# A window attention and Fourier layer over 32 images: image entry, data layout and instruction order redone

## The chip, the cores and the metric

The kernel runs on one core of one Trainium2 chip. The metric is the device time in microseconds (us) of one execution; a lower time is better. TensorE's granted clock is given as a mean over the run, 1.0 being full speed.

## The reference, cut to what matters

```python
# x: (32, 56, 56, 128) fp32, 32 images of 56 x 56 pixels, 128 channels
x = x + attention(group_norm(x), rpb_table, w_qkv, w_proj, b_proj)
x = x + fourier(group_norm(x), w0, w1, W1, b1, W2, b2)

def attention(x):            # Swin, shifted by 3
    xs  = roll(x, (-3, -3))  # windows of 7 x 7, so 8 rows of 8 windows in an image
    q, k, v = windows(xs) @ w_qkv.T           # 4 heads of 32
    a   = softmax(q @ k.T * scale + bias + mask)
    return roll(a @ v @ w_proj.T + b_proj, (3, 3))

def fourier(x):
    xy = idct(mix(dct(x, along width)[:32],  w0))   # 32 modes, a 128x128 matrix for each
    xx = idct(mix(dct(x, along height)[:32], w1))
    return relu((xx + xy) @ W1 + b1) @ W2 + b2       # hidden size 512
```

The attention of an image has to end before its second group norm, and so before its Fourier layer. What can run beside each other is the Fourier layer of one image and the attention of the next. Everything is fp32, and the biases are zeros in the inputs.

## The kernel before

Image entry: transpose 28 pieces, take statistics, then let GpSimd write normalised windows in 27 pieces (cut).

```python
def image_in(b):
    ...                                    # 28 TensorE transposes, ScalarE copies to xT
    rstd, nb = group_stats(st, 0)
    xw = big.tile([P, NWR, NWR, WS, WS], F32, tag="xw", name="xw")
    for i in range(NWR):
        for r0, r1, y0 in rolled(i):
            for j0, j1, s0, s1, x0 in (...):          # the roll cuts the windows
                nc.gpsimd.tensor_scalar(xw[:, i, j0:j1, r0:r1, s0:s1], xT[...], rstd, nb,
                                        ALU.mult, ALU.add)
```

One row of eight windows: K is written into a block-diagonal tile by four copies, each of one head (32 partitions), alternating between ScalarE and VectorE. The score matmul takes all 128 partitions.

```python
    for h in range(NH):
        hs = slice(h * HD, (h + 1) * HD)
        if h % 2:
            nc.vector.tensor_copy(k_bd[hs, :, h], pk3[hs])
        else:
            nc.scalar.copy(k_bd[hs, :, h], pk3[hs])
    ...
    nc.tensor.matmul(ps[half * JP : ..., ...], lhsT=q[:, w * WT : w * WT + JP],
                     rhs=k_bd[:, w].rearrange("c h j -> c (h j)"), ...)   # 196 columns
```

The Fourier layer is a generator whose steps are put between the parts of attention. Columns are made by a GpSimd copy and TensorE transposes (cut):

```python
    for q in range(4):
        nc.gpsimd.tensor_copy(xh[:, ws], xT[:, :, ws].rearrange("p h w -> p w h"))
    for width in (False, True):
        ...                                   # per group: 4 transposes, ScalarE copy, 8 dct matmuls
        nc.vector.tensor_scalar(y[:, 0], y[:, 0], shift, None, ALU.add)
        if width:
            nc.gpsimd.tensor_tensor(xtok, xtok, b2sb..., ALU.add)     # 112 x 3584 at once
        ...                                   # mixing, transposes of z, inverse into xf
    for g in range(NG):                       # feed-forward, 7 groups
        ...

    for b in range(NB):
        attn_scores(xw, 0)
        for i in range(NWR):
            conv = advance(conv, 4)           # 4 steps of the last image's Fourier layer
            if i + 1 < NWR:
                attn_scores(xw, i + 1)
            conv = advance(conv, 4)
            attn_out(xT, i)
        conv = advance(conv, 1000)
        conv = conv_layer(b, xT)
        if b + 1 < NB:
            xT, xw = image_in(b + 1)
```

Of the kernel before, what the change touches and what calls it, by code (L numbers as in the profile page):

```python
# [15 lines left out]
P = 128  # L16
S = 56
C = 128
WS = 7
SS = 3  # L20
NH = 4
# [13 lines left out]
JP = 64  # L35

HALVES = (slice(0, P // 2), slice(P // 2, P))
SQRT_S = float(np.sqrt(float(S)))


@with_exitstack
def swin_fourier_kernel(
# [27 lines left out]
    psum = ctx.enter_context(tc.tile_pool(name="psum", bufs=2, space=bass.MemoryType.PSUM))  # L70

    def bank(tag, bufs):
        return psum.tile([P, 512], F32, tag=tag, name=tag, bufs=bufs)
# [7 lines left out]
    x_tok_src = x.rearrange("b h w c -> b (h w) c").rearrange("b (n p) c -> b p n c", p=TC)  # L81
    out_tok_dst = out.rearrange("b h w c -> b (h w) c").rearrange("b (n p) c -> b p n c", p=TC)


    def load_image(b):
        t = big.tile([TC, NCH, C], F32, tag="xload", name="xload")
        h = NCH // 2
        nc.sync.dma_start(t[:, :h], x_tok_src[b, :, :h])
        nc.sync.dma_start(t[:, h:], x_tok_src[b, :, h:])
        return t  # L90

    loaded = {0: load_image(0)}
# [7 lines left out]
    make_identity(nc, ident)  # L100
    gavg = const_load([P, P], group_avg, "gavg")
    wqkv = const_load([P, 3 * C], w_qkv_t, "wqkv")
    wproj = const_load([P, C], w_proj_t, "wproj")
    bproj = const_load([P, 1], b_proj.rearrange("(c u) -> c u", u=1), "bproj")
# [19 lines left out]
    bm = const.tile([P, 2, 3, NH, WT], F32, tag="bm", name="bm")  # L124
    rpb_f = rpb.rearrange("p h y x -> p h (y x)")
    for r in range(2):
        for s in range(3):
            nc.vector.tensor_tensor(
                bm[:, r, s],
                rpb_f,  # L130
                mask_sb[:, r, s].unsqueeze(1).to_broadcast([P, NH, WT]),
                ALU.add,
            )

    dct_sb = const_load([TC, 2 * NM], dct, "dct")
    w0sb = const_load([P, NM, C], w0, "w0sb")
    w1sb = const_load([P, NM, C], w1, "w1sb")

# [3 lines left out]
    with nc.allow_non_contiguous_dma(reason="constant, once"):  # L142
        for li, ls in enumerate(HALVES):
            nc.scalar.dma_start(idctw[ls], idct_w[ls, li * 2 * S : (li + 1) * 2 * S])
            nc.scalar.dma_start(
                idcth[ls],
                idct_h.rearrange("p (h r) -> p h r", r=4)[ls, :, 2 * li : 2 * li + 2],
            )
    idcth = idcth.rearrange("p h r -> p (h r)")
    wff1 = const_load([P, FF], W1, "wff1")  # L150
# [5 lines left out]


    k_bd = big.tile([P, NWR, NH, WT], F32, tag="k_bd", name="k_bd")
    nc.gpsimd.memset(k_bd, 0.0)
    q_sb, v_bd, a_sb = [], [], []  # L160
    for i in range(2):
        q_sb.append(big.tile([P, RT + JP - WT], F32, tag=f"q{i}", name=f"q{i}"))
        v_bd.append(big.tile([P, NWR, 2, 2, HD], F32, tag=f"v{i}", name=f"v{i}"))
        a_sb.append(big.tile([P, NWR // 2, NH, JP], F32, tag=f"a{i}", name=f"a{i}"))
        nc.gpsimd.memset(q_sb[i], 0.0)
        nc.gpsimd.memset(v_bd[i], 0.0)
        nc.gpsimd.memset(a_sb[i], 0.0)

    def group_stats(st, n):

        mv = small.tile([P, 2], F32, tag="mv", name="mv")
        nc.vector.bn_aggr(mv, st)
        pg = attn_bank() if n == 0 else conv_bank()
# [9 lines left out]
        pv = attn_bank() if n == 0 else conv_bank()  # L183
# [3 lines left out]
        rstd = small.tile([P, 1], F32, tag=f"rstd{n}", name=f"rstd{n}")  # L187
        nc.gpsimd.tensor_tensor(rstd, ve, mhalf, ALU.pow)
        nb = small.tile([P, 1], F32, tag=f"nb{n}", name=f"nb{n}")
# [3 lines left out]
        return rstd, nb  # L193

    def rolled(i):

        y = WS * i + SS
        if i < NWR - 1:
            return ((0, WS, y),)
        return ((0, WS - SS, y), (WS - SS, WS, 0))  # L200


    def image_in(b):

        xl = loaded.pop(b)
        xT = big.tile([P, S, S], F32, tag="xT", name="xT", bufs=2)
        st = small.tile([P, NG, 6], F32, tag="st0", name="st0", bufs=2)
        for g in range(NG):
            pt = attn_bank()
            for i in range(4):  # L210
                nc.tensor.transpose(
                    pt[:, i * TC : (i + 1) * TC], xl[:, 4 * g + i], ident[:TC, :TC]
                )
            nc.vector.bn_stats(st[:, g], pt[:, :GT])
            nc.scalar.copy(
                xT[:, 8 * g : 8 * g + 8].rearrange("p r w -> p (r w)"), pt[:, :GT]
            )
        if b + 1 < NB:
            loaded[b + 1] = load_image(b + 1)
        rstd, nb = group_stats(st, 0)  # L220
        xw = big.tile([P, NWR, NWR, WS, WS], F32, tag="xw", name="xw")
        for i in range(NWR):
            for r0, r1, y0 in rolled(i):
                for j0, j1, s0, s1, x0 in (
                    (0, NWR - 1, 0, WS, SS),
                    (NWR - 1, NWR, 0, WS - SS, S - WS + SS),
                    (NWR - 1, NWR, WS - SS, WS, 0),
                ):
                    cols = (j1 - j0) * (s1 - s0)
                    nc.gpsimd.tensor_scalar(  # L230
                        xw[:, i, j0:j1, r0:r1, s0:s1],
                        xT[:, y0 : y0 + r1 - r0, x0 : x0 + cols].rearrange(
                            "p r (j s) -> p j r s", s=s1 - s0
                        ),
                        rstd,
                        nb,
                        ALU.mult,
                        ALU.add,
                    )
        return xT, xw  # L240


    def attn_scores(xw, i):

        q, v, a = q_sb[i % 2], v_bd[i % 2], a_sb[i % 2]
        src = xw[:, i].rearrange("p j r s -> p (j r s)")
        pq = attn_bank()
        nc.tensor.matmul(pq[:, :RT], lhsT=wqkv[:, 0:C], rhs=src, start=True, stop=True)  # L248
        nc.scalar.mul(q[:, :RT], pq[:, :RT], HD ** (-0.5))
        pk = attn_bank()  # L250
        nc.tensor.matmul(pk[:, :RT], lhsT=wqkv[:, C : 2 * C], rhs=src, start=True, stop=True)
        pk3 = pk[:, :RT].rearrange("p (w j) -> p w j", j=WT)
        for h in range(NH):
            hs = slice(h * HD, (h + 1) * HD)
            if h % 2:
                nc.vector.tensor_copy(k_bd[hs, :, h], pk3[hs])  # L256
            else:
                nc.scalar.copy(k_bd[hs, :, h], pk3[hs])  # L258
        pv = attn_bank()
        wv = wqkv[:, 2 * C : 3 * C].rearrange("c (p h d) -> c h p d", h=2, d=HD)  # L260
# [15 lines left out]
        t = work.tile([P, 2, 2, NH * WT], F32, tag="t", name="t")  # L276
        for hf in range(2):
            ps = attn_bank()
            for w4 in range(4):
                w = 4 * hf + w4  # L280
                half = w % 2
                nc.tensor.matmul(  # L282
                    ps[half * JP : (half + 1) * JP, (w4 // 2) * NH * WT : (w4 // 2 + 1) * NH * WT],
                    lhsT=q[:, w * WT : w * WT + JP],
                    rhs=k_bd[:, w].rearrange("c h j -> c (h j)"),
                    start=True,
                    stop=True,
                )
            nc.vector.tensor_tensor(  # L289
                t[:, hf],  # L290
                ps[:, : 2 * NH * WT].rearrange("p (a m) -> p a m", a=2),
                bm[:, i // (NWR - 1), hf : hf + 2].rearrange("p a h j -> p a (h j)"),
                ALU.add,
            )
        NR = NWR // 2 * NH
        t3 = t.rearrange("p f a (h j) -> p (f a h) j", h=NH)
        a3 = a.rearrange("p a h j -> p (a h) j")[:, :, 0:WT]
        mx = small.tile([P, NR], F32, tag="mx", name="mx")
        nc.vector.tensor_reduce(mx, t3, axis=AX.X, op=ALU.max)  # L299
        nc.gpsimd.tensor_tensor(  # L300
            t3, t3, mx.unsqueeze(2).to_broadcast([P, NR, WT]), ALU.subtract
        )
        nc.scalar.activation(a3, t3, AF.Exp)  # L303
        sm = small.tile([P, NR], F32, tag="sm", name="sm")
        nc.vector.tensor_reduce(sm, a3, axis=AX.X, op=ALU.add)  # L305
        rs = small.tile([P, NR], F32, tag="rs", name="rs")
        nc.vector.reciprocal(rs, sm)  # L307
        nc.gpsimd.tensor_tensor(a3, a3, rs.unsqueeze(2).to_broadcast([P, NR, WT]), ALU.mult)  # L308

    def attn_out(xT, i):  # L310

        v, a = v_bd[i % 2], a_sb[i % 2]
        po = attn_bank()
        for hf in range(2):
            pt = attn_bank()
            for m in range(4):
# [3 lines left out]
                    a[:, pr, 2 * hp : 2 * hp + 2].rearrange("p h j -> p (h j)"),  # L320
# [4 lines left out]
            for w4 in range(4):  # L325
                w = 4 * hf + w4
                for hp in range(2):
                    nc.tensor.matmul(  # L328
                        po[hp * JP : (hp + 1) * JP, w * WT : (w + 1) * WT],
                        lhsT=v[:, w, hp].rearrange("j h d -> j (h d)"),  # L330
                        rhs=aT[:, 2 * (w4 // 2) + hp, w % 2, 0:WT],
                        start=True,
                        stop=True,
                    )
# [263 lines left out]
```

## Time and profile before

| | before |
|---|---|
| time, median of 3 runs | 6233.24 us (6227.3 to 6234.22) |
| granted clock | 0.895 |
| period of one image in the steady stage | 191.15 us |
| TensorE between matmuls, idle, per image | 31.3 us |
| VectorE, ScalarE, GpSimd busy | 41%, 41%, 26% |

The period is the distance between the starts of the same row of two images that follow each other, a mean over the middle of the run. The idle time is the sum of the gaps between the end of one matmul and the start of the next. Both are worked out from the records of the trace. A group's columns are: line, engine, operation, output and inputs, shape, count, then busy us in total and mean ns, then the idle us before it and what ended most of it. First, groups of the kernel before.

```profile
L282 PE MATMUL pa<-k_bd,q 128*64 128x196 f32 x4096 | 491.5, 373 | 325.0 <-DVE k_bd L256 325.0
L256 DVE COPY k_bd<-pa 32x392 f32<-32x392 f32 x512 | 289.4, 565 | 762.6 <-ACT k_bd L258 759.7
```

TensorE's longest waits in the kernel before (us in total, times, longest us):

```profile
PE pa L282 <- DVE k_bd L256: 325.0, 194, 6.5
PE pc L419 <- DVE y L407: 213.8, 33, 8.0
```

The score matmuls wait for VectorE's part of K. In most rows VectorE's part waits in turn for ScalarE's: the four copies run one after the other. But 194 of the 325 us are 31 waits of 6.2 to 6.5 us, one at the entry of each later image. The prediction shows one of them, before 3056.74. VectorE's timeline there:

```profile
3055.74 0.16 DVE L190 SCALAR_TENSOR_TENSOR nb<-gm,rstd 128x1 f32<-128x1 f32 x1 [6.71 <-POOL rstd L188]
3055.93 0.15 DVE L364 TENSOR_SCALAR shift<-nb 128x1 f32<-128x1 f32 x1
3056.12 0.57 DVE L256 COPY k_bd<-pa 32x392 f32<-32x392 f32 x1
```

VectorE stands 6.71 us in a step of the second group norm, which waits for GpSimd behind its pass of windows, and makes its last copy of K only after it. The mode mixing waits for a VectorE add of 56 columns. Together these two are 539 of the run's 6234 us.

### The profile page before, as it was taken

Reading aid. Unit: us, or ns where it says so; the run is one execution under the profiler, and the core shown is the slowest. Engines: PE = TensorE matmul, PEld = TensorE weight load, DVE = VectorE, ACT = ScalarE, POOL = GpSimd, SP = SyncE. Lnnn points to the kernel's source line nnn. Section 1 sums busy time; section 2 is a strip of 40 time slices with the busy share of each in tenths; the row PEclk is TensorE's granted clock in tenths of the full one; section 3 lists DMA queues with packets and bytes.
Section 4 is the critical chain, followed back from the end, with each engine's and each line's share of the span. In section 5 each row is a group of like instructions: output and inputs, shape, how many; then the busy total and the mean of one; then the engine's idle time right before and its main releaser. Section 6 shows DMA issues by size and latency. Waiting matters only on the chain.

```text
span 6234.4 us, 133310 instructions
## 1 busy us (share of the span) xinstructions
PE 5145.8 (83%) x59392; PEld 3814.3 (61%) x59392; DVE 2544.2 (41%) x4487; ACT 2566.0 (41%) x4961; POOL 1640.8 (26%) x1614
## 2 busy tenths in 40 slices
PE   5888888788888888887888888888888888888887
PEld 3666666566665666665666656666666666566665
DVE  3443444443444434444334344344443443443441
ACT  2444344443444443444434444434444344443343
POOL 2232212322223322133222232222222222322211
PEclk8888899888998898998989988989889899888897
DMA  2000000000000000000000000000000000000000
GB/s 57 16 18 22 22 12 19 16 20 22 22 12 15 19 22 22 12 18 16 22 22 21 11 16 19 22 22 12 16 18 22 22 14 17 16 20 22 12 12 11
DMA packets 217976, 116.79 MB, mean 19 GB/s; under 512 B 15255, under 2 KB 217016, under 8 KB 217144
## 3 DMA queue, kind: packets, MB, share of 16 engines
q1 hardware_dynamic: 206136, 102.84, 7.0%
q8 instruction: 466, 7.63, 0.5%
q10 hardware_dynamic: 11264, 5.42, 0.4%
q14 instruction: 110, 0.90, 0.1%
HBM read 56.82 MB, written 51.38 MB: 17 GB/s over the span
## 4 chain that ended last, share of the span: by engine, by line
PE 59%; DVE 17%; POOL 12%; ACT 9%; issue 2%; DMA 0%; SPq 0%; ACTq 0%; POOLq 0%; DVEq 0%
PE pc L496 12%; PE pc L482 8%; PE pa L282 7%; POOL xw L230 6%; POOL t L300 5%; PE pc L419 4%; DVE y L407 4%; PE pc L392 4%; PE pa L328 3%; PE pa L341 3%; PE pc L381 3%; DVE mx L299 3%; PE pa L248 3%; ACT a L303 3%; PE pa L318 3%; PE pc L451 3%
## 5 line engine op out<-in xcount | busy, mean ns | idle before, releaser
L300 POOL TENSOR_TENSOR t<-t,mx 128x784 f32<-128x784 f32 x256 | 384.7, 1503 | 3202.3 <-DVE mx L299 3189.6
L496 PEld LDWEIGHTS pc<-wff,hid 128*112 128x112 f32 x7168 | 847.7, 177 | 177.3 <-ACT hid L490 83.5
L496 PE MATMUL pc<-wff,hid 128*112 128x128 f32 x7168 | 913.2, 276 | 27.4 <-ACT hid L490 24.1
L490 ACT ACTIVATE hid<-pc,b1sb 128x448 f32<-128x448 f32 x896 | 550.3, 633 | 673.9 <-PE pc L482 638.6
L282 PE MATMUL pa<-k_bd,q 128*64 128x196 f32 x4096 | 491.5, 373 | 325.0 <-DVE k_bd L256 325.0
L482 PE MATMUL pc<-xf,wff 128*128 128x448 f32 x1792 | 732.1, 542 | 0.0
L256 DVE COPY k_bd<-pa 32x392 f32<-32x392 f32 x512 | 289.4, 565 | 762.6 <-ACT k_bd L258 759.7
L282 PEld LDWEIGHTS pa<-k_bd,q 128*64 128x64 f32 x4096 | 329.3, 154 | 408.5 <-DVE k_bd L256 304.5
L308 POOL TENSOR_TENSOR a<-a,rs 128x784 f32<-128x784 f32 x256 | 389.2, 1520 | 700.6 <-DVE rs L307 307.5
L328 PE MATMUL pa<-aT,v 128*64 128x49 f32 x8192 | 391.5, 241 | 126.4 <-DVE aT L324 122.7
L324 DVE COPY aT<-pa 128x512 f32<-128x512 f32 x512 | 352.1, 688 | 344.6 <-PE pa L318 344.2
L289 DVE TENSOR_TENSOR t<-pa,bm 128x392 f32<-128x392 f32 x512 | 290.0, 567 | 477.0 <-PE pa L282 469.7
L328 PEld LDWEIGHTS pa<-aT,v 128*64 128x64 f32 x8192 | 320.9, 151 | 236.9 <-DVE aT L324 159.8
L504 DVE TENSOR_TENSOR xtok<-pc,xtok 112x512 f32<-112x512 f32 x224 | 153.9, 687 | 723.1 <-PE pc L496 723.1
L482 PEld LDWEIGHTS pc<-xf,wff 128*128 128x128 f32 x1792 | 313.6, 191 | 221.1 <-issue 202.7
L305 DVE TENSOR_REDUCE sm<-a 128x16 f32<-128x784 f32 x256 | 248.3, 970 | 370.7 <-ACT a L303 370.7
L303 ACT ACTIVATE a<-t 128x784 f32<-128x784 f32 x256 | 223.0, 871 | 428.3 <-POOL t L300 423.8
L401 ACT ACTIVATE y<-pc,rstd 128x256 f32<-128x256 f32 x448 | 211.0, 471 | 451.6 <-PE pc L392 293.4
L346 DVE SCALAR_TENSOR_TENSOR xT<-pa,bproj,xT 128x371 f32<-128x371 f32 (+2 forms) x576 | 200.2, 394 | 467.2 <-PE pa L341 464.4
L318 PE MATMUL pa<-ident,a 128*128 128x128 f32 x2048 | 368.9, 302 | 26.2 <-POOL a L308 26.2
L230 POOL TENSOR_SCALAR xw<-xT,rstd,nb 128x343 f32<-128x343 f32 (+7 forms) x864 | 373.2, 454 | 11.9 <-DVE ve L186 11.5
L419 PE MATMUL pc<-y,w0sb 128*64 128x56 f32 x4096 | 197.4, 271 | 213.0 <-DVE y L407 213.0
(78 smaller groups left out, 7848.2 us busy)
## 6 DMA issues: line engine op xcount, KB each, us to landing
xload<-in_x_dram SPq DMA_DIRECT2D x64, 784.0 KB
out_dram<-xtok SPq DMA_DIRECT2D x224, 224.0 KB
w0sb<-in_w_dram ACTq DMA_DIRECT2D x1, 2048.0 KB
w1sb<-in_w_dram ACTq DMA_DIRECT2D x1, 2048.0 KB
wff<-in_W_dram ACTq DMA_DIRECT2D x2, 256.0 KB
rpb<-in_rpb_rev_dram ACTq DMA_DIRECT2D x25, 0.8 KB
rpb<-in_rpb_rev_dram SPq DMA_DIRECT2D x24, 0.8 KB
wqkv<-in_w_qkv_t_dram ACTq DMA_DIRECT2D x1, 192.0 KB
```

Source lines behind the costliest of these rows:

```text
L230: nc.gpsimd.tensor_scalar(xw[:, i, j0:j1, r0:r1, s0:s1], xT[:, y0 : y0 + r1 - r0, x0 : x0 + cols].rearrange("p r (j s) -> p j r s", s=s1 - ...
L282: nc.tensor.matmul(ps[half * JP : (half + 1) * JP, (w4 // 2) * NH * WT : (w4 // 2 + 1) * NH * WT], lhsT=q[:, w * WT : w * WT + JP], rhs=k_ ...
L300: nc.gpsimd.tensor_tensor(t3, t3, mx.unsqueeze(2).to_broadcast([P, NR, WT]), ALU.subtract)
L303: nc.scalar.activation(a3, t3, AF.Exp)
L308: nc.gpsimd.tensor_tensor(a3, a3, rs.unsqueeze(2).to_broadcast([P, NR, WT]), ALU.mult)
L318: nc.tensor.transpose(pt[:, m * P : (m + 1) * P], a[:, pr, 2 * hp : 2 * hp + 2].rearrange("p h j -> p (h j)"), ident,)
L324: nc.vector.tensor_copy(aT.rearrange("p m a j -> p (m a j)"), pt)
L328: nc.tensor.matmul(po[hp * JP : (hp + 1) * JP, w * WT : (w + 1) * WT], lhsT=v[:, w, hp].rearrange("j h d -> j (h d)"), rhs=aT[:, 2 * (w4 / ...
L419: nc.tensor.matmul(pz[hs, c * S : (c + 1) * S], lhsT=wmix[:, k, hs], rhs=y[:, k], start=True, stop=True,)
L482: nc.tensor.matmul(ph[:, :GT], lhsT=wff1[:, f * P : (f + 1) * P], rhs=xf[:, 8 * g : 8 * g + 8].rearrange("p r w -> p (r w)"), start=True, ...
L490: nc.scalar.activation(hf, ph[:, :GT], AF.Relu, bias=b1sb[:, f : f + 1])
L496: nc.tensor.matmul(pf[:TC, c * C : (c + 1) * C], lhsT=hid[f][:, c * TC : (c + 1) * TC], rhs=wff2[:, f], start=(f == 0), stop=(f == NF - 1),)
```

## The change

The intent is to keep TensorE busy: no stage without Fourier work, no pass of GpSimd over the image, fewer transposes, and smaller score matmuls. The core of the diff:

```diff
 # 1 rolled frame: the image is loaded rolled, and transposed straight into windows
-                    nc.gpsimd.tensor_scalar(xw[:, i, j0:j1, r0:r1, s0:s1], xT[...], rstd, nb, ...)
+            nc.tensor.transpose(pt4[:, :, 2 * c : 2 * c + 2], im.x[:, WS * i // 2 + c], ident_x[...])
+        nc.scalar.copy(xw.rearrange("p (j t) -> p j t", t=WT), mine)
 # 2 norm in the weights
+        nc.scalar.mul(im.w, wqkv, rstd)
+        ...                                   # bias = wqkv.T @ nb, three one-column matmuls
 # 3 token-major projection: the output lands as tokens, one residual add for each row of windows
-        nc.tensor.matmul(pp[:, :RT], lhsT=wproj, rhs=oT, start=True, stop=True)
+            nc.tensor.matmul(pp[:TC, ...], lhsT=oT[:, ...], rhs=wproj, start=True, stop=True)
 # 4 columns via DRAM
-            nc.gpsimd.tensor_copy(xh[:, ws], xT[:, :, ws].rearrange("p h w -> p w h"))
-                    nc.tensor.transpose(pt[:TC, ...], tokens[:, n * TC : (n + 1) * TC], ident)
+        nc.sync.dma_start(im.scr[2 * n0 : 2 * n1]..., piece)          # after each attention row
+                nc.sync.dma_start(t[r * S : (r + 1) * S], src[r, :, CH * g : CH * (g + 1)])
 # 5 scores: 16 matmuls of 98 columns on 64x64 tiles in place of 8 of 196 on 128x64
-                    lhsT=q[:, w * WT : w * WT + JP],
-                    rhs=k_bd[:, w].rearrange("c h j -> c (h j)"),
+                    lhsT=q[cs, w * WT : w * WT + JP],
+                    rhs=k_bd[cs, w].rearrange("c h j -> c (h j)"),
 # 6 the small adds
-            nc.vector.tensor_scalar(y[:, 0], y[:, 0], shift, None, ALU.add)
+            nc.scalar.activation(y[:, 0], y[:, 0], AF.Identity, bias=shift)
-                nc.gpsimd.tensor_tensor(xtok, xtok, b2sb..., ALU.add)  # 112 x 3584
+            nc.gpsimd.tensor_tensor(res, res, b2sb..., ALU.add)        # 112 x 512, seven times
 # 7 order: Fourier layer of image b spread evenly over 8 rows of image b+1; image b+1 enters in rows 3 to 6
-        conv = advance(conv, 1000)
-            xT, xw = image_in(b + 1)
+        share = PE_CONV / NWR / 2 if R >= NWR + LAG else 0.0
+        if T_BEGIN < i < NWR - 1 and b + 1 < NB:
+            ...                               # image_group(images[b + 1], g)
+        advance(share)
```

Line numbers shift: the scores are L282 before and L324 after, the inverse transform L451 and L555, the forward transform L392 and L479, the two feed-forward matmuls L482 and L496 before, L602 and L619 after.

## The prediction

> **What bounds the kernel now.** I read the page first (busy shares, slices, chain), then stages of one image, then the timeline inside the bad stages, then the waits.
>
> ```profile
> PE 5145.8 (83%) x59392; PEld 3814.3 (61%) x59392; DVE 2544.2 (41%) x4487; ACT 2566.0 (41%) x4961; POOL 1640.8 (26%) x1614
> ...
> PEclk8888899888998898998989988989889899888897
> ...
> PE 59%; DVE 17%; POOL 12%; ACT 9%; issue 2%; DMA 0%; SPq 0%; ACTq 0%; POOLq 0%; DVEq 0%
> ```
>
> TensorE leads in busy time and holds 59% of the chain, but 41% of the chain is elsewhere, and its clock is never full on average. VectorE and ScalarE are at 41%: no second engine is near a limit. So the question is how much of a period TensorE does nothing, or runs at half clock. From the start of one image's window row to the same row of the next image is 191.1 us (3044.9 to 3236.5 is one such period). Cut into stages (columns: window, length, busy us of PE, PEld, DVE, ACT, POOL, then granted clock, DMA):
>
> ```profile
> 3014.00:3062.00 48.00, 30.68 (x267) 21.85 (x267) 20.78 (x46) 12.77 (x24) 22.87 (x36) 0.69 0.18 39
> 3062.00:3114.00 52.00, 47.24 (x788) 35.20 (x788) 22.22 (x39) 34.02 (x73) 11.42 (x8) 0.99 0.01 2
> 3114.00:3124.00 10.00, 3.21 (x64) 2.71 (x60) 7.94 (x2) 1.72 (x4) 7.73 (x1) 0.84 0.00 0
> 3124.00:3206.00 82.00, 79.03 (x780) 58.67 (x778) 29.05 (x55) 32.10 (x57) 9.07 (x6) 0.98 0.07 18
> ```
>
> Stage 1 (48 us): the Fourier layer of the last image has run out, attention's last rows run alone, then the next image is transposed, normalised and cut into windows. A quarter of the period at clock 0.69. Stage 3 is one stall of 7 us. Stages 2 and 4, attention beside the Fourier layer, are dense at full clock. The timeline shows what stages 1 and 3 wait for:
>
> ```profile
> 3043.53 11.66 POOL L230 TENSOR_SCALAR xw<-xT,rstd,nb 128x343 f32<-128x343 f32 x27 [0.37 <-DVE ve L186]
> ...
> 3056.74 2.88 PE L282 MATMUL pa<-k_bd,q 128*64 128x196 f32 x16 [6.19 <-DVE k_bd L256]
> ...
> 3114.57 7.73 POOL L409 TENSOR_TENSOR xtok<-xtok,b2sb 112x3584 f32<-112x3584 f32 x1 [5.57 <-PE pc L392]
> ...
> 3114.99 7.37 DVE L407 TENSOR_SCALAR y<-y,shift 128x56 f32<-128x56 f32 x1 [0.18 <-ACT y L401]
> ...
> 3122.41 1.85 PE L419 MATMUL pc<-y,w0sb 128*64 128x56 f32 x30 [6.61 <-DVE y L407]
> ```
>
> GpSimd spends 11.7 us making windows, the second statistics' power queues behind it, and TensorE stands for 6.2 us. Later a 56-element VectorE add takes 7.37 us because a 7.7 us GpSimd add runs beside it; TensorE stands for 6.6 us.
>
> **TensorE's own work.** I took warm costs from back-to-back groups in the timeline (one matmul shows as two instructions): Q or K projection 0.66 us, the 16 value matmuls 1.03, the 8 score matmuls 1.48, an attention transpose 0.112, 8 attention-times-value matmuls 0.60, output projection 0.75; per image also 28 input transposes 2.9 and statistics 0.9. A row of attention is 1.32+1.03+1.48+0.90+1.20+0.75 = 6.68 us, 53.4 for 8. The Fourier layer: 56 transposes 6.2, cosine transform 8.5, mode mixing 8.4, transposes back 3.9, inverse 7.7, first feed-forward matmuls 28 x 0.752 = 21.1, second 112 x 0.22 = 24.6; together 80.4. Sum 137.6 us. So 191.1 - 137.6 = 53.5 us per image are stalls and half clock. Measuring the rows by the starts of their Q projections: rows 7 and 0 (no or little Fourier work, image entry) last 51.5 us for 22.6 of work; row 4 (the stall) 28.8 for 16.1; rows 2 and 3 34.3 for 29.1, a ratio of 1.18; rows 5 and 6 (feed-forward) 61.8 for 58.4, a ratio of 1.06. Those two ratios are my tools for the new kernel.
>
> **What the Trainium skill says.** "TensorE: Matmul & The Clock Gate", Part 1, says that the array's clock drops to half after an idle window of about 3.4 us and returns after a busy one. The trace agrees: the granted clock is 0.50 from 3025 to 3035 us, and transposes there take 1.11 us for four against 0.60 warm. "SBUF — State Buffer", section "Who interferes with whom", says that a VectorE copy or scalar op in its two-port mode and GpSimd block each other for a whole instruction. The 7.37 us add agrees (its shortest run is 0.25 us). "TensorEngine Tiling (Array Packing)", "Available Configurations" and "Gotcha 1", lets four 64x64 tiles run at once, different row tiles in different PSUM banks. The trace agrees: the inverse transform, 64x64 tiles, does 8 matmuls of 112 columns in 0.55 us, while the 8 attention-times-value matmuls of only 49 columns on 128x64 tiles need 0.60. "DMA: Bandwidth & Descriptors", "Anatomy of one DMA", puts the fixed cost of a DMA at about 2 us, mostly the write receipt; the page of this case gives no landing times, so that stays unchecked.
>
> **The change, part by part, per image.**
> 1. Rolled frame. The image is loaded already rolled, transposed straight into windows (32 transposes x 0.11 = 3.5 us against 2.9), and ScalarE copies them out. GpSimd's 27 window instructions (864 over 32 images, 392 us, 12.2 per image) go.
> 2. Norm in the weights: one 128x384 scaling on ScalarE, three one-column matmuls (0.7 us), biases inside copies that exist anyway. No pass over the pixels.
> 3. Token-major projection: 28 matmuls x 0.22 = 6.2 us against 6.0. Residual adds become one per row, and ScalarE squares plus two VectorE reductions per row (about 16 x 0.6 = 10 us VectorE, 8 x 0.6 = 5 us ScalarE, estimates by the durations of same-size operations) replace statistics over channel-major pixels.
> 4. Columns via DRAM: all 56 Fourier transposes (6.2 us TensorE) go, with their 14 ScalarE copies (262 us over the run, 8.2) and GpSimd's transposing copy (205.8, 6.4). DMA gains three passes of 3136 packets of 512 bytes per image; at the 34 ns per packet worked out from 7.0% of 16 engines for 206136 packets, the queue's share rises to about 20%. Not a bound.
> 5. Scores on 64x64 tiles: 16 x 98 columns; by the inverse's 0.55 us for 8 x 112 this is 0.96 us against 1.48.
> 6. The 3.8 us add goes to ScalarE and the 7.7 us add is cut into seven: stage 3 goes.
> 7. Order: images are prepared in rows 3 to 6 of the image before, and the Fourier layer of image b is spread over exactly eight rows of image b+1. Stage 1 goes. The instruction order of the built kernel confirms it: every steady row has both, with 14 to 19 us of TensorE work by the costs above.
>
> TensorE work: row 1.32+1.03+0.96+0.90+1.35 (18 matmuls, cut edge window)+0.77 = 6.33, x 8 = 50.6; preparation 4.6; Fourier layer 80.4 - 6.2 + 0.4 = 74.6. Sum 129.8: only 7.8 us less. The gain is in the 53 us of stalls. Rows 1 to 3 (transform, mixing, inverse) hold 45.6 us by the order listing, at 1.18 = 53.8. The other five hold 84.2, and I take 1.08, not 1.06, since attention is denser there: 90.9. Period 144.7 us.
>
> The others per image, by the rows of the page, removals and additions as above: VectorE 79.5 to about 80, ScalarE 80 to about 81, GpSimd 51 to about 41. At most 56% of the period.
>
> Whole run: entry 55 us (first Q projection is at 54.7 now; constants are loaded as before). Nine rows without Fourier work: 58.6 us of TensorE work at half clock (such rows last 11.6 to 13.6 us now for 6.7) = 117. Then 247 rows, 247/8 x 144.7 = 4468. Tail: one and an eighth Fourier layers alone. Now the one takes 140 us (6091 to 6234); without the transpose-copy-transform ping-pong, the 8 us add stall and GpSimd's copy I put it at 100. Sum 4740; I say 4750.
>
> **Rivals.**
> A: the losses inside a row persist everywhere. Scores still wait for the four alternating ScalarE and VectorE copies of K (325 us of TensorE idling for that wait), inverse matmuls for ScalarE's copies. Then 1.18 holds for all rows: 129.8 x 1.18 = 153 per period, total about 5000. Against it: in rows 5 and 6 the scheduler hid these waits under feed-forward matmuls.
> B: the DRAM trip is exposed: column loads queue on the one SyncE queue behind stores and the next image, GpSimd waits in order for the residual's load and holds the softmax. 5 us per image would make 4900. Against it: one row of lag, two loads ahead, residuals fetched a group ahead.
> C: dense packing works as in rows 5 and 6 everywhere: 129.8 x 1.06 = 137.6, total about 4520.
> D: little gain, since an in-order ScalarE or VectorE with two more operations per row sets the pace. At 56% I hold this unlikely; it would need a row of 23 us for no gain.
>
> **Range and chances.** C and A bound most of it; B adds to A. 8 in 10: 4570 to 5000. Even A and B together stay 15% faster, so faster by over 2% has 0.97, within 2% 0.02, slower 0.01.
>
> **What would show it.** The granted clock near full in all middle slices; PE busy near 90% or above; PE instructions up; no GpSimd group with 128x343 or 112x3584; a period near 145 us; the score group's spacing under 1 us for 16; GpSimd and SyncE waits on DMA short. I am wrong if VectorE or ScalarE lead the chain of waits, if TensorE waits on column tiles, or if score matmuls do not overlap across row tiles (then 0.5 us more per row, 4 per image).

## The result, and the profile after

The kernel after took 4984.91 us (median of 4 runs, 4968.27 to 4992.51), against 6233.73 us for the kernel before in the same rounds. The ratio is 0.7994, with a 95% interval of 0.7973 to 0.8016. Ratios here are the mean time of one kernel's fast runs over that of the other's of the same rounds, so not quite the ratio of the medians. The predicted time was 4750 us with a range up to 5000: inside, near the top.

The page of the kernel after: busy times, granted clock in 40 slices, and the chain of work that ended last, by engine.

```profile
PE 4641.3 (93%) x64320; PEld 3587.0 (72%) x64320; DVE 2428.6 (49%) x4469; ACT 2491.8 (50%) x4705; POOL 1385.5 (28%) x1071
...
PEclk8799999999999999999999999999999999999999
...
q1 hardware_dynamic: 521272, 257.03, 20.3%
...
PE 72%; DVE 10%; ACT 7%; POOL 5%; issue 3%; DMA 2%; ACTq 1%; SPq 0%; POOLq 0%; DVEq 0%
```

TensorE went from 83% to 93% busy, from 59% to 72% of the chain, and the dips of the clock are gone but for the first two slices. Stages of the kernel after (window, length, busy us of PE, PEld, DVE, ACT, POOL, then granted clock, DMA share, GB/s): the nine rows before the first Fourier layer, the steady stage, the tail, and one period out of the middle.

```profile
61.00:204.00 143.00, 106.88 (x1064) 80.02 (x1064) 69.74 (x119) 45.49 (x78) 39.25 (x29) 0.67 0.05 14
204.00:4841.00 4637.00, 4408.77 (x61870) 3408.82 (x61870) 2319.46 (x4264) 2390.61 (x4519) 1316.15 (x1006) 0.99 0.22 55
4841.00:4980.00 139.00, 116.64 (x1348) 89.91 (x1346) 26.64 (x53) 50.28 (x98) 15.00 (x12) 0.93 0.18 50
2302.00:2453.00 151.00, 143.75 (x2020) 111.19 (x2020) 75.54 (x139) 78.03 (x149) 43.09 (x33) 0.99 0.21 55
```

The period fell from 191.15 to 151.02 us. TensorE's gaps per image fell from 31.3 to 7.3 us: this alone is 24 of the 40 us. Time at half clock fell from 38.5 to 3.7 us per image; the rest is this and less work.

But the period should have been 144.7. The scores are the first place to look. A group line, then the timeline of TensorE in one row (start, us, engine, line, operation, count; one fp32 matmul shows as two instructions). The group of the kernel after:

```profile
L324 PE MATMUL pa<-k_bd,q 64*64 64x98 f32 x8192 | 420.8, 252 | 16.6 <-DVE k_bd L297 13.7
```

Timeline of the kernel after, TensorE alone:

```profile
3016.59 1.02 PE L602 MATMUL pc<-xf,wff 128*128 128x448 f32 x2
3017.53 0.89 PE L324 MATMUL pa<-k_bd,q 64*64 64x98 f32 x16
3018.36 1.02 PE L602 MATMUL pc<-xf,wff 128*128 128x448 f32 x2
3019.30 0.89 PE L324 MATMUL pa<-k_bd,q 64*64 64x98 f32 x16
...
3041.55 0.61 PE L555 MATMUL pc<-idctw,zT 64*64 64x112 f32 x16
3042.09 0.47 PE L619 MATMUL pc<-wff,hid 128*112 128x128 f32 x2
```

The wait for K has nearly gone, from 325 to 14 us. But this row has two groups of 16 instructions, and each takes 0.83 us (3017.53 to 3018.36), 1.66 us for the row. The inverse, also on 64x64 tiles and with more columns, does 16 instructions in 0.54 us (3041.55 to 3042.09). The built order of instructions tells why. The first group is the eight matmuls of partitions 0 to 63, which can start once two K copies are done. The second is the eight of partitions 64 to 127. Inside a group only two tiles of the array are in use, so two instructions start in each 84 ns. In the inverse four tiles follow each other, and four instructions start in each 93 to 96 ns. In six of the eight rows of an image the halves stay apart as here. In the other two, matmuls of both halves come together, and the scores of the row take 0.99 and 1.14 us.

TensorE's longest waits in the kernel after (the start-up wait aside), and one of GpSimd's:

```profile
POOL res L596 <- DMA res<-scr: 837.5, 165, 43.8
...
PE pc L555 <- ACT zT L550: 119.2, 138, 1.5
PE pc L479 <- DMA htok<-scr: 42.9, 31, 2.7
```

These three name the other suspects: the inverse waits for a ScalarE copy of turned modes (zT, the mixed modes after TensorE has transposed them), the column transform for its load from DRAM, and GpSimd for the residual's load.

### The profile page after: what moved, and what is told of

It reads as the page before. It is cut to its first block, busy times and chain, and to the rows that moved or that the text cites. A ratio compares the mean times of both kernels' runs of the same rounds, so it can differ in the third digit from the quotient of the medians.

```text
span 4980.0 us, 143896 instructions
## 1 busy us (share of the span) xinstructions
PE 4641.3 (93%) x64320; PEld 3587.0 (72%) x64320; DVE 2428.6 (49%) x4469; ACT 2491.8 (50%) x4705; POOL 1385.5 (28%) x1071
## 3 DMA queue, kind: packets, MB, share of 16 engines
q1 hardware_dynamic: 521272, 257.03, 20.3%
## 4 chain that ended last, share of the span: by engine, by line
PE 72%; DVE 10%; ACT 7%; POOL 5%; issue 3%; DMA 2%; ACTq 1%; SPq 0%; POOLq 0%; DVEq 0%
PE pc L619 14%; PE pc L602 11%; PE pa L324 6%; PE pa L379 6%; PE pc L526 5%; PE pa L304 5%; POOL a L346 5%; PE pa L400 5%; PE pc L555 5%; PE pa L286 4%; PE pa L291 3%; DVE mx L345 3%; PE pa L365 2%; ACT a L349 2%; PE pa L230 2%
## 5 line engine op out<-in xcount | busy, mean ns | idle before, releaser
L619 PE MATMUL pc<-wff,hid 128*112 128x128 f32 x7168 | 926.5, 283 | 0.7 <-ACT hid L610 0.6
L619 PEld LDWEIGHTS pc<-wff,hid 128*112 128x112 f32 x7168 | 840.8, 182 | 55.1 <-issue 14.6
L346 POOL TENSOR_TENSOR a<-a,mx 128x784 f32<-128x784 f32 x256 | 389.0, 1519 | 1700.2 <-DVE mx L345 1586.2
L602 PE MATMUL pc<-xf,wff 128*128 128x448 f32 x1792 | 781.1, 553 | 0.8 <-DVE xf L582 0.8
L297 DVE TENSOR_SCALAR k_bd<-pa,bqkv 32x392 f32<-32x392 f32 x512 | 320.7, 626 | 619.8 <-ACT k_bd L299 613.7
L596 POOL TENSOR_TENSOR res<-res,b2sb 112x512 f32<-112x512 f32 x224 | 284.8, 1271 | 859.2 <-DMA res<-scr 837.5
L337 DVE TENSOR_TENSOR a<-pa,bm 128x392 f32<-128x392 f32 x512 | 284.8, 567 | 408.2 <-PE pa L324 403.5
L324 PE MATMUL pa<-k_bd,q 64*64 64x98 f32 x8192 | 420.8, 252 | 16.6 <-DVE k_bd L297 13.7
L324 PEld LDWEIGHTS pa<-k_bd,q 64*64 64x64 f32 x8192 | 327.4, 133 | 143.4 <-DVE k_bd L297 85.3
L379 PE MATMUL pa<-aT,v 128*64 128x49 f32 (+2 forms) x9216 | 386.8, 227 | 35.7 <-DVE aT L371 33.5
L602 PEld LDWEIGHTS pc<-xf,wff 128*128 128x128 f32 x1792 | 300.4, 190 | 164.5 <-issue 91.8
L304 PEld LDWEIGHTS pa<-wn,xw 128*49 128x49 f32 x8192 | 258.8, 125 | 161.6 <-issue 63.4
L242 POOL TENSOR_TENSOR xl<-xl,bproj 112x384 f32<-112x384 f32 (+1 forms) x256 | 285.2, 1136 | 237.8 <-PE pa L230 234.3
L313 ACT COPY v<-pa 49x512 f32<-49x512 f32 x512 | 293.3, 573 | 78.0 <-PE pa L304 72.4
```

Of the source, the lines that this page charges most:

```text
L297: nc.vector.tensor_scalar(dst, pk3[hs], im.bias[hs, 1:2], None, ALU.add)
L304: nc.tensor.matmul(pv[hh * JP : hh * JP + WT, w * JP : (w + 1) * JP], lhsT=src[:, w * WT : (w + 1) * WT], rhs=wv[:, hh], start=True, stop= ...
L324: nc.tensor.matmul(ps[hp][qs, (w // 2) * 2 * WT : (w // 2 + 1) * 2 * WT], lhsT=q[cs, w * WT : w * WT + JP], rhs=k_bd[cs, w].rearrange("c h ...
L346: nc.gpsimd.tensor_tensor(a3, a3, mx2.unsqueeze(2).to_broadcast([P, 2 * NR, WT]), ALU.subtract)
L379: nc.tensor.matmul(po3[hp * JP : (hp + 1) * JP, :, x0 : x0 + s1 - s0], lhsT=v[:, w, hp].rearrange("j h d -> j (h d)"), rhs=aT[:, 2 * (w4 / ...
L602: nc.tensor.matmul(ph[:, :GT], lhsT=wff1[:, f * P : (f + 1) * P], rhs=xf[:, 8 * g : 8 * g + 8].rearrange("p r w -> p (r w)"), start=True, ...
```

## The experiments

Periods and idle times below are worked out as above. "After" is 4985 us, period 151.0, ratio 0.7994. All twelve kernels gave the right result but for one. In the rounds of the first four runs the kernel before took 6221.66 us, in the others 6232 to 6235; so a difference of medians to "after" can be off by some 12 us in those four, and the ratios decide.

### The scores: which order, which tiles

**Four tiles next to each other.** The edit orders the 16 matmuls and ties each to the one before it, so that the built order keeps them together:

```diff
-        for w in range(NWR):
-            for hp in range(2):
+        for w2 in range(NWR // 2):
+            for hp, half in ((0, 0), (0, 1), (1, 0), (1, 1)):   # second run: (0,0),(1,0),(0,1),(1,1)
+                # ... and an order-only dependency of each matmul on the one before it
```

> The 16 score matmuls of a row are kept together in the order row tile 0 with both column tiles, then row tile 1 with both. Theory T (the scheduler parted the two row tiles, so only two of four tiles run at once; that is most of why the period is 151.0 us and not 144.7): the scores fall from about 1.68 us a row to about 1.0, 5 us an image, so about 4830 us (4800 to 4870). Rival W (TensorE waits for other engines inside the row, its own time does not count): within 1% of 4985.

> Same, but in the order of the source: both row tiles of one column tile, then both of the other. T in its plain form (any four different tiles overlap): as the run with the other order, 4800 to 4870. If instead neighbours must lie in different columns to overlap, no gain over 4985.

Measured: 4906.47 us (ratio 0.7903, 0.7875 to 0.7931) and 4869.14 us (0.7822, 0.7807 to 0.7836). The second is just inside the 4800 to 4870 that I expected, the first outside it and also outside the rival's. Timeline of the second, TensorE's scores of one row and the group that follows:

```profile
3011.40 0.38 PE L326 MATMUL pa<-k_bd,q 64*64 64x98 f32 x2
...
3013.20 0.90 PE L326 MATMUL pa<-k_bd,q 64*64 64x98 f32 x30
...
3014.03 0.69 PE L631 MATMUL pc<-wff,hid 128*112 128x128 f32 x4
```

Thirty instructions in 0.83 us, in the time that sixteen took. So the tiles do overlap across the two halves of the partitions, with either alternation, and the kernel after loses this by its order alone. But look at the waits of this second run:

```profile
PE pa L326 <- DVE k_bd L297: 92.1, 76, 2.8
...
PE pc L567 <- ACT zT L562: 63.0, 78, 1.5
```

The wait for K is back, 92 us against 14, because the group is now held together: its first matmul starts early (the x2 at 3011.40), but the other fifteen start only after the last of the four copies. From the start of each score matmul to the start of the next matmul there are now 11.2 us per image, 2.5 of them idle, in place of 13.7, of which 1.9 are idle (two groups per image are followed by a wait for turned modes). Without the idle time that is 8.7 against 11.8, where a bare 0.83 us for a row would be 6.6: part of what the packing wins goes into a new wait. The period is 147.6. Taken in tile order (first run) the time is 37 us longer; TensorE's wait for attention's transposes (aT) is 130 us there against 81, but why the two orders differ, with the same packing, was not settled.

**Scores as before.** All the rest of the change, but eight matmuls of 196 columns over 128 partitions, with the layouts of K and of the attention tile that go with it (some small buffers cut to fit).

```diff
-                    lhsT=q[cs, w * WT : w * WT + JP],
-                    rhs=k_bd[cs, w].rearrange("c h j -> c (h j)"),      # 16 of 98 columns
+                    lhsT=q[:, w * WT : w * WT + JP],
+                    rhs=k_bd[:, w].rearrange("c h j -> c (h j)"),       # 8 of 196 columns
```

> Undoes the score part alone: 8 matmuls of 196 columns on 128x64 tiles as before, K with zeros for the other heads. T: the tiling earned nothing, 1.48 us a row against 1.68, so within 1% of 4985 (4920 to 5000). If the tiling had earned what was predicted, 0.5 us a row, it would be 130 us slower (5115).

Measured: 5069.29 us (0.8148, 0.8136 to 0.816), 84 us slower than after (96 by the ratios) and outside what I expected. I had held that both forms cost nearly the same because the kernel after gets no concurrency from its tiles. They do not: TensorE's wait for K is the difference.

```profile
PE pa L321 <- DVE k_bd L294: 182.9, 131, 3.4
```

183 us against 14. The scores take 11.7 us of an image here, none of it idle, as much as the kernel after without its idle time (11.8). But TensorE is idle for 12.6 us per image against 7.3, and the period is 153.6. The loss would be larger if half clock in the steady stage had not fallen, from 113 to 17 us. So part 5 of the change did earn its place, not by running four tiles at once but by the shorter wait for K. That half of the scores can start after two copies is what the timeline shows; the layouts changed with it.

### The two DRAM loads

**Residual add removed.** The bias is zero, so the result stays right.

```diff
-            nc.gpsimd.tensor_tensor(res, res, b2sb.unsqueeze(1)..., ALU.add)
```

> GpSimd's add of the output bias to the reloaded residual taken out (the bias is zero in these inputs, so the result stays right). GpSimd stands 837 us in that line for the load. Rival B (this wait holds the softmax and through it TensorE): 2% faster or more, under 4890. T: the wait is slack, within 1% of 4985.

Measured: 4980.32 us (0.8002, 0.7984 to 0.802): the same as after. GpSimd's 837 us of waiting for that load disappear and the time does not move. GpSimd, 28% busy, waits elsewhere instead: its wait for the row maximum of the softmax (mx) grows from 1586 to 2371 us. This fells the half of rival B that had GpSimd hold up the softmax.

**Columns not loaded.** The column transform reads the row chunks in place of the loads from DRAM. Its output is wrong, which doesn't matter for the time. (Relative error 0.455.)

```diff
         def col_chunks(g):
-            if g + 2 < NCH // CH:
-                cols[g + 2] = col_load(g + 2)
-            return cols.pop(g)
+            return im.x[:, CH * g : CH * (g + 1)]
```

> The changed kernel with the column transform reading the row tokens in SBUF in place of the columns reloaded from DRAM; the result is wrong on purpose. Rival B (the DRAM trip is exposed): the page shows 43 us of TensorE idling for these loads, and a half-clock window often follows that stage, so 1 to 2% faster, 4890 to 4935. If the trip is hidden: within 0.5% of 4985.

Measured: 4929.48 us (0.7907, 0.7893 to 0.792), so the trip through DRAM costs about 55 us, or 1.7 us per image. The waits named it with 43. In the traces TensorE's idle time falls by 25 us in all, as another wait grows (attention's transposes, 34 to 48 us), and its time at half clock by 69 us, which is worth up to 35. Timeline of the kernel after at one of these waits, then the window that follows it:

```profile
2186.19 0.66 PE L365 MATMUL pa<-ident,a 128*128 128x128 f32 x4
2189.29 1.76 PE L479 MATMUL pc<-dct_h,htok 112*64 112x64 f32 x28 [2.45 <-DMA htok<-scr]
2190.81 1.07 PE L379 MATMUL pa<-aT,v 128*64 128x49 f32 x16
```

```profile
2188.70:2195.53 6.83, 6.24 (x98) 5.85 (x100) 1.82 (x3) 2.40 (x4) 1.94 (x3) 0.50 0.39 84
2195.60:2202.40 6.80, 6.80 (x135) 5.34 (x131) 2.15 (x4) 4.04 (x8) 1.10 (x1) 1.00 0.14 36
```

In the first window, which begins 0.6 us before the wait ends, the clock is 0.50, and the 16 attention-times-value instructions take 1.07 us against 0.67 elsewhere. TensorE is "busy" for 91% of that window: a busy share does not show a half clock. In the steady stage the kernel after has 30 such windows, 113 us in all; without the column loads 18 remain, 65 us. So other waits cause them too.

### Where the gain comes from: old and new parts under old and new order

**New parts, order of before.** The image enters after the last row, the Fourier layer is done before the row after it starts; loads are kept early.

```diff
+        share = PE_CONV / 6.4 / 2 if b else 0.0
+        for i in range(NWR):
+            advance(share); attn_scores(im, i + 1); advance(share); attn_out(im, i)
+        advance(1e9)
+        convs.append(conv_layer(images.pop(b)))
+        ...                                  # image_group x 8, image_norm, attn_scores(.., 0)
```

> All new parts, but the order of before: the Fourier layer is used up in 6.4 rows, then the last rows of attention run alone, then the next image is transposed and normalised. Theory O (the gain is mostly the overlap of every row with Fourier work): the quarter without Fourier work comes back at half clock, about 158 us a period, 5260 us in all (5150 to 5400), and the clock dips. Rival G (the gain is mostly the GpSimd and VectorE work that was removed): within 1% of 4985.

Measured: 5655.67 us (0.9074, 0.906 to 0.9087), well above what I expected. The page's clock line shows the dips of the kernel before again:

```profile
PEclk8888998888998889988899888899888998888998
```

Its period is 172.95 us at a granted clock of 0.897. With the same instructions, the order alone is worth 5656 - 4985 = 671 us here.

**Old parts, small adds only.** The 56-column add goes to ScalarE and the big GpSimd add is cut into seven, in the kernel before.

```diff
-            nc.vector.tensor_scalar(y[:, 0], y[:, 0], shift, None, ALU.add)
+            nc.scalar.activation(y[:, 0], y[:, 0], AF.Identity, bias=shift)
-                nc.gpsimd.tensor_tensor(xtok, xtok, b2sb..., ALU.add)
+                for g in range(NG):
+                    nc.gpsimd.tensor_tensor(piece, piece, b2sb..., ALU.add)
```

> The kernel before with one part alone: the 56-element add on ScalarE and the 7.7 us GpSimd add cut into seven. If the stall of 6.6 us is gone and nothing takes its place: 6.6 to 8 us x 32 less, 5970 to 6020 us. Rival (TensorE then waits for the next thing in the stage): over 6150.

Measured: 5913.24 us (0.9482, 0.9466 to 0.9498), 320 us or 10 us per image from two lines. The stall that it takes away was 6.6 us of idle time per image in the kernel before; I expected that and little more. The clock rose from 0.895 to 0.916. In the traces idle time falls by 199 us and time at half clock by 320 us, worth up to 160: some of the gain is half clock after the stall.

**Old parts, order of after.** The Fourier layer's 51 steps are spread over the 16 half rows of the next image, and the next image enters at row 4 (window buffer doubled, one hidden buffer fewer).

```diff
+            if i == 4 and b + 1 < NB:
+                nxt = image_in(b + 1)
+            for part in range(2):
+                to = STEPS * (2 * i + part + 1) // (2 * NWR)
+                conv = advance(conv, to - int(done[0]))
```

> The kernel before with the new order alone: Fourier steps spread evenly over eight rows, the next image entered in row 4, its first scores before the last row ends (window tile doubled, one hidden-layer buffer fewer). O: 137.6 us of TensorE work at a ratio of about 1.17, plus the 7 us stall and some wait for GpSimd's windows: about 170 us a period, 5620 us (5450 to 5750). G: little gain, over 6000.

Measured: 5864.02 us (0.9405, 0.9391 to 0.9419), 370 us, less than I expected (5450 to 5750 us in all). The wait for K falls from 325 to 57 us by the order alone (of the long waits none over 5 us is left), but the stall of the small add stays. TensorE's waits in this run:

```profile
PE pc L419 <- DVE y L407: 233.7, 64, 8.0
...
PE pa L282 <- DVE k_bd L256: 57.3, 70, 4.9
```

**Both.**

> The kernel before with two parts alone, the new order and the two small adds. If the two are worth their sum: 320 + 370 us, 5540 us (5500 to 5590), and the new data path (frame, norm in the weights, columns by DRAM, tokens) makes the other 560. If GpSimd's windows and copies stand in the way of the order, over 5650.

The edit is the two diffs above together. Measured: 5697.89 us (0.9137, 0.9122 to 0.9152). The two parts gain 536 us together, less than the 690 of their sum; the figure I expected, 5540, was the sum, and the rival (above 5650, because the old parts keep getting in each other's way) held. The longest wait of TensorE there is new:

```profile
PE pc L453 <- ACT zT L446: 216.6, 171, 5.0
```

It was 82.9 us in the kernel before and is 119.2 in the kernel after. In this run ScalarE still has the 14 transposing copies of each image.

The four runs and the two kernels make a ladder. Where parts overlap, their share depends on what is already there:

| kernel | median us | period us |
|---|---|---|
| before | 6233 | 191.2 |
| + small adds | 5913 | 180.9 |
| + order | 5864 | 178.8 |
| + both | 5698 | 174.1 |
| new parts, old order | 5656 | 173.0 |
| after | 4985 | 151.0 |

With the old parts, order and adds give 536 us; the new data path on top gives 5698 - 4985 = 713. With the old order, everything else gives 577; the order on top gives 671. With the small adds in place, the data path is worth 258 us under the old order (5913 - 5656) and 713 under the new. The data path and the order need each other. My reading, argued and not shown by itself: under the new order nearly every transpose and wait that the new data path saves lies on TensorE's path, while under the old one many fall into stages that are long for other reasons.

### A better version

**K in two copies.** On top of the second score order, K is written by two full-width operations, which multiply by 0 or 1 for each partition, one on ScalarE and one on VectorE.

```diff
-        for h in range(NH): ...               # four copies of 32 partitions
+        nc.scalar.activation(k_bd[:, :, 0], pk3, AF.Identity, bias=im.bias_k[:, 0:1], scale=heads[:, 0:1])
+        nc.vector.tensor_scalar(k_bd[:, :, 1], pk3, heads[:, 1:2], im.bias_k[:, 1:2], ALU.mult, ALU.add)
```

> Scores in the source's tile order, and K written by two full-width operations with a 0/1 scale per partition in place of four 32-partition ones. Theory K (with the tiles together, what is left of the score stage is the wait for the four K copies one after another, 2.5 us idle and some 4 us hidden in slots per image): about 6 us an image less than 4869, so 4660 to 4750. Rival (the wait moves to other operands, ScalarE and VectorE free time is no help): within 1% of 4869.

Measured: 4885.0 us (0.7835, 0.7823 to 0.7847), against 0.7822 for the kernel that it builds on. The scores fall to 7.7 us per image and the wait for K to 9 us in all. The time does not fall, as the rival said, since the waits moved. TensorE's waits in this run:

```profile
PE pc L571 <- ACT zT L566: 117.1, 169, 2.3
...
PE pc L495 <- DMA htok<-scr: 56.3, 31, 4.7
```

The wait for turned modes is up from 63 to 117 us and that for columns from 4 to 56, and half clock in the steady stage is 249 us against 68. The built order of instructions changed with the edit; that it puts less work into those gaps is my reading, which no run isolates.

**Turned modes a group ahead.** On top of the second score order, with the four K copies: the transposes of z and the ScalarE copy for inverse group g+1 are issued before the matmuls of group g.

```diff
+            zT = ahead
+            if g + 1 < NG:
+                ahead = turn(zh, g + 1)       # 2 transposes and the ScalarE copy
-            px = back(zh, g, idcth)
+            px = back(zT, idcth)              # the same for zw / idctw
```

> Scores in the source's tile order, and in the inverse transform the transposes and ScalarE copy of the next group issued one group ahead of the matmuls that need them. Theory F (stalls between dependent small stages are what is left, also the cause of half-clock windows): TensorE's wait for the ScalarE copy (1.9 us an image idle and some in slots) goes: 4870 falls to 4760 to 4830. Rival (order does not matter, TensorE work is the bound): within 0.5% of 4870.

Measured: 4771.22 us (4770.08 to 4777.92; ratio 0.7657, 0.7644 to 0.7669), the best of all, and right. Page and waits of this run:

```profile
PE 4524.0 (95%) x64320; PEld 3477.7 (73%) x64320; DVE 2442.7 (51%) x4469; ACT 2451.4 (51%) x4705; POOL 1388.3 (29%) x1071
...
PE 79%; DVE 11%; ACT 4%; POOL 3%; issue 2%; DMA 1%; SPq 0%; ACTq 0%; POOLq 0%; DVEq 0%
```

```profile
PE pa L326 <- DVE k_bd L297: 16.4, 17, 2.3
...
PE pc L570 <- ACT zT L562: 0.5, 2, 0.3
```

The wait for turned modes is gone, and with it most of the wait for K (16 us against 92); that the scores now find other work ahead of them is my reading. Idle time is 4.4 us per image, half clock 41 us in the steady stage, the period 144.53.

**Both.** The same edit on top of the two K copies.

> Both: two K copies, scores in tile order, transposes a group ahead. The two-K kernel has 335 us at half clock in its trace against 178 without, mostly after the stage that waits for the transposed copy. F: these windows go too and the K gain shows: 4650 to 4780. Rival: 4870 to 4890 as its parts.

Measured: 4838.96 us (0.7761, 0.775 to 0.7773), 68 us slower than with four copies, and outside both ranges that I had named. TensorE's longest wait in this run:

```profile
PE pa L395 <- DVE aT L387: 145.3, 197, 2.1
```

Scores are at their shortest here, 6.9 us per image, but attention waits longer between its transposes and its values (145 us against 78), the columns wait 50 us against 3, and half clock is 171 us. That the build's order puts less work into these gaps fits; which step of it does so stays open.

## Why the prediction was right or wrong, point by point

**Direction, size and place.** Right. Stages 1 and 3 went, the clock filled up, TensorE reached 93% and no second engine came near a limit: in the period shown, VectorE has 75.5 us, ScalarE 78 and GpSimd 43, where about 80, 81 and 41 were predicted. DMA's share was predicted as about 20% and is 20.3%. Of the signs named, three went the other way: 16 scores are not spaced under 1 us but take 1.66 us in most rows, GpSimd's waits on DMA are not short (837 us), and TensorE does wait on column tiles (43 us).

**Why 4985 and not 4740, the sum.** By its own terms:

| term | predicted us | measured us | off by |
|---|---|---|---|
| start of the first Q projection | 55 | 60.9 | +6 |
| nine rows without Fourier work | 117 | 142.8 | +26 |
| 247 rows | 4468 | 4663 (247/8 x 151.0) | +195 |
| tail | 100 | 113 | +13 |
| sum | 4740 | 4980 | +240 |

**The period.** The step that failed is "The other five hold 84.2, and I take 1.08". Measured row by row in the kernel after, with the same warm costs, rows 1 to 3 last 53.7 us for 45.6 of work: 1.18, as assumed. The other five last 97.3 for 84.3: 1.15. This is 6.4 us, the whole of the 6.3 that the period is off. The 1.08 was the 1.06 of rows 5 and 6 of the kernel before, where the waits hid under feed-forward matmuls, with a little added for denser attention. In the kernel after these five rows exceed their work by 13 us: some 3.4 are idle and 2.7 are scores above the 0.96 us counted, beside 2 us at half clock; the rest was not apportioned.

**The term inside it: the scores.** Part 5 took 0.96 us for a row from the inverse's packing. Measured, they take 13.7 us per image in place of 7.7; 1.9 of the 13.7 is idle time after them, so the term itself is 4.1 us too small. The condition was named at the end of the prediction ("if score matmuls do not overlap across row tiles"), with 4 us per image as its price, and that price was right; I had not looked at the order in which the build puts the 16 matmuls. The runs show that the hardware does overlap them (30 instructions in 0.83 us), and that the wait for K stands against it: without overlap the shorter wait was worth 96 us by the ratios (full rows against half rows), and with overlap the wait came back, which left a gain of 107. To have both, the wait for turned modes had to go as well. With both mended the period is 144.53, against 144.7 predicted, and the time 4771 against 4750. It is not a match line by line: the scores take 8.5 us there, not 7.7, and the head is as long as in the kernel after.

**The nine rows.** Predicted as TensorE work at half clock. The granted clock there was 0.67, and still they took 26 us more: TensorE is busy 107 of the 143 us, and waits in the rest: a row of attention with no Fourier work beside it has nothing to fill the gaps between its own copies. The two-copy run passes these rows in 121 us (61.4 to 182.7), so the copies of K are likely part of that wait.

**The rivals.** A, that row losses persist everywhere, named 153 us and about 5000, and is nearest to what happened; its cause was half right. The wait for K did not persist in the kernel after, the wait for turned modes did (119 us). The 325 us that A put down to the four copies were misread: 194 of them were the long waits behind GpSimd's windows, a pass that the change removes. B was mis-sized: 55 us in all for the columns, not 5 us per image, and nothing for the residual. C and D fell.

**What the parts are worth.** The prediction laid nearly the whole gain to stalls and to the order. The ladder shows that order and small adds alone reach 5698, and that the new data path on top of them brings 713 us. Its counted savings per image (transposes 6.2 us) are only a part of the 23 us that separate the two periods; idle time is 11.4 us of it (18.8 against 7.3), and time at half clock in the steady stage falls from 546 to 113 us, worth up to 7 us per image. So what the data path brings is again mostly stalls and half clock, as the prediction had it for the whole. Part 6 has one slip: its "3.8 us add" is the mean of 32 adds of 0.25 us and 32 of about 7.3.

## What to carry to other kernels

Count what a tiled group costs from the order in which the build issues it, not from the shape: independent tiles help only where neighbours in the order use different ones, and a group that is kept together waits for the last of its inputs. When a wait is taken away in a statically ordered kernel, rerun the list of waits before counting the gain, since the order changes with it and the next copy becomes the wait; starting such a copy a group ahead was worth more here than making it shorter. Measure an order and a data path together as well as alone: here each was worth far more with the other in place.

## What the Trainium skill lacked or had wrong

- "TensorEngine Tiling (Array Packing)", "Key Properties": it says that tiles execute in parallel, not that neighbours in issue order have to use different ones. Here eight 64x64 matmuls on two tiles took 0.83 us, and fifteen on four tiles took the same 0.83 us. (Part 3 of "TensorE: Matmul & The Clock Gate" comes nearest, for weight loads; no run here separates the number of tiles from which rows of the array they use.)
- "TensorE: Matmul & The Clock Gate", Part 1: it ties the half clock to an idle window. Here half clock began within a gap of 2.45 us, and in this stretch of 6.8 us at 0.50 the profile counts TensorE busy for 91%; in the kernel before, TensorE was busy for 70% of 3025 to 3035 us, all at 0.50. How little activity counts as idle is not on the page: 30 such windows, 113 us, fell into a stage that reads as 95% busy, and in the 3.4 us before each of them TensorE was busy for 38 to 74%.
- "DMA: Bandwidth & Descriptors": no figure there is for such a load of columns, in packets of some 500 bytes (257 MB in 521272 packets) between other transfers on SyncE's queue, and no view of the profile gives the time from its issue to its landing. What a trip through DRAM costs when two loads run ahead had to be measured by leaving it out: 55 us of 4985.
